# A graph layer's edge loop: TensorE's five steps in another order

## The chip, the cores and the metric

The kernel runs on one core of one Trainium2 chip. A core has five engines that run side by side, each through its own list of instructions in order: TensorE (PE; its weight loads are listed as PEld) multiplies matrices and writes to PSUM, VectorE (DVE) and ScalarE (ACT) do elementwise work, GpSimd (POOL) issues here the gathers by index, and SyncE (SP) issues the plain transfers. The metric is the time of one execution on the device in microseconds, as the median of several runs.

## The reference, cut to what matters

One layer of a graph transformer in float32: a message passing branch over 53,125 directed edges of 3,125 nodes with 256 features each, a linear attention branch, and a top-2 mixture of eight experts behind a second layer norm. The change touches the message passing branch alone. Cut to the terms that are not dropped, it computes:

```python
s0, s1 = _lin(x0[src], x1[src], ls0, ls1)          # gather of the source node
h0, h1 = _fctp(s0, s1, sh1, t1_00, t1_11, t1_01, t1_10)
h0, h1 = _lin(h0, h1, lh0, lh1)
sc = leaky_relu(h0) @ lsc * INV_MUL
act = softmax(concatenate([sc, zeros(E, 3 * 64)]))
o0, o1 = _fctp(h0, h1, sh1, t2_00, t2_11, t2_01, t2_10)
msgs = act * concatenate([o0, o1.reshape(E, 3 * 64)])
agg = segment_sum(msgs, dst)
```

The edges come sorted by destination. `sh1` is the unit vector of the edge, scaled.

## The kernel before, in words

Ahead of the loop the kernel normalises the nodes, folds the weight matrices into `wab` (first layer), `wo` (edge products) and `lsc` (second layer), and writes a table with one row of 448 numbers for each node. The edge loop (function `edges`) then works on 416 tiles of 128 edges, four tiles to a group, 104 groups. Behind it the expert blocks run, with TensorE as the busy engine.

For one group g the steps are:

- `gather` (L790, GpSimd): four indirect transfers fetch the rows of 4 x 128 source nodes into `xg`. There are seven `xg` buffers; one comes free when the group's sums are done.
- `features` (L813 to L815, VectorE): the dot product of the gathered vectors with the edge directions. Its last instruction is kept as `READY_[g]`.
- `places` (L798, L803, VectorE): 0/1 matrices `place` that say to which of 64 slots of a window of destinations each edge belongs; every third group also `move`, which carries a window into the next.
- `turn` (L820 TensorE, L822 ScalarE): four transposes into the PSUM tile `pz`, and a copy to `zT`.
- `products` (L830, L834, L838): the first layer `ph` on TensorE, from `zT` and `wab`, with 64 columns of the array for each half of the group; `little`, a scaled copy of it by ScalarE; and the edge products `eo`, four full multiplications of `zT` with `wo`. There are two `eo` buffers and one of `ph`.
- `second_layer` (L844, L850): VectorE takes the maximum `low` of `ph` and `little`, the leaky relu, and TensorE multiplies it with `lsc` to the scores `sc`, with 64 rows of the array for each half.
- `scores` (L858, L860): the minimum `nm` on VectorE, the exponentials `ex` and their sum on ScalarE.
- `messages` (L869 to L891): on VectorE the reciprocal `z` of the sum and the weight `zero` of the constant part; on ScalarE four scalings of `place` by `zero` into `zplace` (L876); on VectorE `oplace` (L878), and then the messages `msg` (L888 and L891), which read `eo`.
- `sums` (L914, L917, L921): TensorE adds `msg` and part of `xg` into the window's sum, with `oplace` and `zplace` as stationary matrices of 64 columns; in the last group of a window it also adds the part carried over from the window before (L921), ScalarE copies the first half of the sum out, and SyncE stores it to `agg` in memory.
- `second` (L937): in the last group of a window, TensorE carries from the first half to the second, which is copied out and stored in turn.

Pass s of the loop writes out, in this order: the gather of group s+3, the sums of s-3, one or two parts of side work (attention, and the routing of nodes to experts), the scores of s-2, features, places and transposes of s, the second layer of s-1, the messages of s-2, the products of s, and `second` of s-3. A planner turns this into one list for each engine: it takes the earliest written instruction that is ready by its own estimate of times, so that the lists can differ from the written order. `tc.issue_after(x)` pins the instructions of its block behind x in the list of their engine. The waits between engines follow from the data and the buffers.

Two such pins set TensorE's order before: the first layer of g comes behind the second layer of g-1 (`LSC[g - 1]`), and the second layer of g behind the transposes of g+1 (`TURN[g + 1]`). VectorE's pins put `low` of g behind the features of g+1 and the weight `z` of g behind `low` of g+1.

## Time and profile before

| what | value |
|---|---|
| median of 3 runs | 1110.63 us (1109.84 to 1115.06) |
| profiled execution | 1108.81 us |
| its span in the profile | 1106.9 us |
| edge loop in the span | from about 67 us (first gather) to 697 us |
| TensorE busy | 1018.8 us, 92% of the span |
| VectorE busy | 698.7 us, 63% |
| ScalarE busy | 500.6 us, 45% |
| GpSimd busy | 630.3 us, 57% |

A row of instructions in the profile gives the line of the kernel, the engine, the operation, the tile written and the tiles read, the shape and the number of instructions; behind the first bar the time they filled together and the mean of one in nanoseconds; behind the second the idle time of the engine just ahead of them and what ended it. On TensorE the shape begins with the part of the array in use: `128*64` is 128 rows by 64 columns. In the timelines the columns are start, length, engine, line, operation, tiles, shape and count, neighbouring instructions of one line being merged; the end of a matmul is modelled, so that it can lie behind the start of the next. In the table of stretches each engine has its busy time and its number of instructions, followed by the clock granted to TensorE, the busy share of the transfer engines, and GB/s.

### The profile page before, as it was taken

Reading aid. Unit: us, or ns where it says so; the run is one execution under the profiler, and the core shown is the slowest. Engines: PE = TensorE matmul, PEld = TensorE weight load, DVE = VectorE, ACT = ScalarE, POOL = GpSimd, SP = SyncE. Lnnn points to the kernel's source line nnn. Section 1 sums busy time; section 2 is a strip of 40 time slices with the busy share of each in tenths; the row PEclk is TensorE's granted clock in tenths of the full one; section 3 lists DMA queues with packets and bytes.
Section 4 is the critical chain, followed back from the end, with each engine's and each line's share of the span. In section 5 each row is a group of like instructions: output and inputs, shape, how many; then the busy total and the mean of one; then the engine's idle time right before and its main releaser. Section 6 shows DMA issues by size and latency. Waiting matters only on the chain.

```text
span 1106.9 us, 21729 instructions
## 1 busy us (share of the span) xinstructions
PE 1018.8 (92%) x7616; PEld 812.5 (73%) x7616; DVE 698.7 (63%) x2177; ACT 500.6 (45%) x1861; POOL 630.3 (57%) x623
## 2 busy tenths in 40 slices
PE   3848999999999999999999899899999999999996
PEld 3726776766667776776667676688888888888885
DVE  5987899988898989988888987322671111111110
ACT  3714556665576665765566545223211223222221
POOL 4447777777777776777766751432534434445322
PEclk9958999999999999999999899899999999999998
DMA  5945665667766686766766542765653667676651
GB/s 161 334 126 158 181 184 164 176 177 236 207 173 184 183 240 190 200 170 174 214 179 188 161 136 101 273 195 166 215 181 119 200 194 256 215 231 187 188 170 20
DMA packets 73882, 204.95 MB, mean 185 GB/s; under 512 B 13163, under 2 KB 48549, under 8 KB 70181
## 3 DMA queue, kind: packets, MB, share of 16 engines
q0 software_dynamic: 40736, 171.18, 52.9%
q1 hardware_dynamic: 31135, 30.40, 8.2%
q10 hardware_dynamic: 1894, 1.89, 0.5%
q8 instruction: 63, 1.03, 0.4%
q14 instruction: 54, 0.44, 0.1%
HBM read 176.00 MB, written 27.84 MB: 184 GB/s over the span
## 4 chain that ended last, share of the span: by engine, by line
PE 70%; DVE 12%; DMA 6%; issue 4%; POOL 3%; ACT 3%; SPq 0%; DVEq 0%; POOLq 0%; ACTq 0%
PE ps L1300 15%; PE ps L1318 15%; PE ps L917 8%; PE eo L838 7%; DMA xg<-table,srcT 4%; PE ph L830 4%; PE pz L820 3%; PE ps L914 3%; PE sc L850 3%; POOL xg L790 3%; PE gp L646 2%; PE gp L1095 2%; DVE tmp L813 2%; DVE msg L888 1%; PE ps L937 1%
## 5 line engine op out<-in xcount | busy, mean ns | idle before, releaser
L790 POOL DMA_INDIRECT xg<-table,srcT x416 | 441.1, 1060 | 163.5 <-issue 108.1
L876 ACT ACTIVATE zplace<-place,zero 128x64 f32<-128x64 f32 x416 | 115.3, 339 | 71.9 <-DVE zero L873 71.8
L838 PE MATMUL eo<-wo,zT 128*128 128x128 f32 x832 | 122.5, 292 | 25.3 <-DVE msg L891 24.9
L1305 ACT ACTIVATE hT<-ps,wt 128x256 f32<-128x256 f32 (+1 forms) x144 | 57.8, 453 | 194.3 <-issue 122.0
L838 PEld LDWEIGHTS eo<-wo,zT 128*128 128x128 f32 x832 | 105.4, 197 | 52.5 <-DVE msg L891 37.0
L860 ACT ACTIVATE ex<-sc,nm 128x65 f32<-128x65 f32 x416 | 125.5, 317 | 13.3 <-DVE nm L858 7.1
L1300 PE MATMUL ps<-xt,wt 128*128 128x256 f32 (+1 forms) x576 | 121.7, 368 | 4.4 <-DVE y L1321 4.4
L1318 PE MATMUL ps<-wt,hT 128*128 128x256 f32 x528 | 117.3, 379 | 0.0
L1300 PEld LDWEIGHTS ps<-xt,wt 128*128 128x128 f32 x576 | 103.4, 194 | 17.5 <-DVE y L1321 4.8
L813 DVE TENSOR_TENSOR tmp<-xg,r 128x768 f32<-128x768 f32 x104 | 98.7, 949 | 18.8 <-DMA xg<-table,srcT 15.4
L1318 PEld LDWEIGHTS ps<-wt,hT 128*128 128x128 f32 x528 | 98.8, 190 | 12.6
L917 PE MATMUL ps<-xg,zplace 128*64 128x192 f32 x832 | 107.5, 336 | 0.0
L1231 DVE COPY xt<-psx 128x512 f32<-128x512 f32 (+1 forms) x27 | 17.6, 651 | 140.1 <-PE psx L1230 133.2
L822 ACT COPY zT<-pz 128x512 f32<-128x512 f32 x104 | 60.7, 584 | 86.7 <-PE pz L820 85.1
L1323 POOL DMA_INDIRECT out_dram<-y,ridx_late x32 | 51.0, 1594 | 76.8 <-DVE y L1321 48.8
L917 PE MATMUL ps<-msg,zplace 128*64 128x192 f32 x692 | 91.4, 342 | 0.0
L860 ACT ACTIVATION_READ_ACCUMULATOR ex<-sc,nm 128x1 f32 x416 | 86.3, 208 | 0.0
L1323 POOL DMA_INDIRECT out_dram<-y,ridx_early x20 | 32.3, 1614 | 87.9 <-DVE y L1321 33.6
L820 PE MATMUL pz<-ident,xg 128*128 128x128 f32 x416 | 69.6, 288 | 10.4 <-DVE xg L815 8.1
L914 PE MATMUL ps<-msg,oplace 128*64 128x64 f32 (+1 forms) x832 | 78.4, 268 | 0.6 <-DVE msg L891 0.6
L820 PEld LDWEIGHTS pz<-ident,xg 128*128 128x128 f32 x416 | 45.3, 143 | 41.3 <-issue 32.9
L830 PE MATMUL ph<-zT,wab 128*64 128x256 f32 x416 | 69.0, 409 | 6.0 <-ACT zT L822 3.0
(383 smaller groups left out, 1898.3 us busy)
## 6 DMA issues: line engine op xcount, KB each, us to landing
xg<-table,srcT POOLq DMA_INDIRECT x416, 3.7
table<-xt SPq DMA_DIRECT2D x4, 1120.0 KB
agg<-win SPq DMA_DIRECT2D x70, 64.0 KB
agg<-zero SPq DMA_DIRECT2D x1, 3200.0 KB
x<-in_x_dram SPq DMA_DIRECT2D x2, 768.0 KB
at<-agg SPq DMA_DIRECT2D x2, 768.0 KB
out_dram<-x SPq DMA_DIRECT2D x2, 768.0 KB
rows<-at SPq DMA_DIRECT2D x2, 768.0 KB
```

The lines of the kernel that those rows point to most:

```text
L790: nc.gpsimd.indirect_dma_start(out=XG[g][:, i, :], out_offset=None, in_=table[:, :], in_offset=bass.IndirectOffsetOnAxis(ap=srcT[:, j:j + ...
L813: nc.vector.tensor_mul(tmp, xg[:, :, U:D].rearrange("p g (m u) -> p g m u", m=3), rbc(g))
L820: TURN[g] = nc.tensor.transpose(pz[:, i, :], XG[g][:, i, 0:P], ident)
L830: nc.tensor.matmul(ph[h * U:(h + 1) * U, :], lhsT=wab, rhs=zT[:, 2 * h:2 * h + 2, :].rearrange("p t e -> p (t e)"), start=True, stop=True)
L838: nc.tensor.matmul(eo[:, t, :], lhsT=zT[:, t, :], rhs=wo, start=True, stop=True)
L860: nc.scalar.activation(ex[:, i, :], sc[:, i, 0:U + 1], AF.Exp, scale=-1.0, bias=nm[:, i:i + 1], accum_out=z[:, i:i + 1])
L876: nc.scalar.activation(zero_place[:, i, :], place[:, i, :], AF.Copy, scale=zero[:, i:i + 1])
L914: nc.tensor.matmul(ps[hs, 0:c1], lhsT=one_place[:, i, :], rhs=msg[:, i, 0:c1], start=whole, stop=False)
L917: nc.tensor.matmul(ps[hs, U:D], lhsT=zero_place[:, i, :], rhs=msg[:, i, U:D] if what == 1 else xg[:, i, D:TW], start=False, stop=False)
L1300: nc.tensor.matmul(ps[:, h, 0:W_], lhsT=w[:, k * HID + cc * P:k * HID + (cc + 1) * P], rhs=xT[:, k, 0:W_], start=(k == 0), stop=(k == 1))
L1318: nc.tensor.matmul(ps, lhsT=hT[:, cc, s * P:(s + 1) * P], rhs=w[:, o:o + D], start=(cc == 0), stop=(cc == NC - 1))
L1323: nc.gpsimd.indirect_dma_start(out=out[:, :], out_offset=bass.IndirectOffsetOnAxis(ap=ridx[q][:, at_], axis=0), in_=y[:, s, :], in_offset= ...
```

## The change

TensorE's cycle becomes: sums of s-3, first layer and edge products of s-1, transposes of s, second layer of s-1, `second`. For that `products` moves from group s to group s-1 and ahead of `turn`; the first layer of g is pinned behind the last sum of g-2 (`SUMS`), the edge products behind the first layer, the transposes of g behind the edge products of g-1 (`WO`), and `second` of g behind the second layer of g+2. `messages` is split: the weights with `oplace` and `zplace` are now a function `weights`, written ahead of `products`; the messages proper stay behind the second layer. On VectorE `z` of g is pinned behind the features of g+2, `low` of g behind `oplace` of g-1 (`PLACED`), and the messages of g behind `low` of g+1 as before. `places` moves to the end of the pass. The diff, shortened:

```diff
             def turn(g):
                 pz = zps.tile([P, G, P], F32, name="pz")
-                for i in range(G):
-                    TURN[g] = nc.tensor.transpose(pz[:, i, :], XG[g][:, i, 0:P], ident)
+                with tc.issue_after(WO[g - 1].ins) if g else nullcontext():
+                    for i in range(G):
+                        TURN[g] = nc.tensor.transpose(pz[:, i, :], XG[g][:, i, 0:P], ident)
...
                 for h in range(2):
-                    with tc.issue_after(LSC[g - 1].ins) if g and not h else nullcontext():
-                        nc.tensor.matmul(ph[h * U:(h + 1) * U, :], lhsT=wab,
+                    with tc.issue_after(SUMS[g - 2].ins) if g >= 2 and not h else nullcontext():
+                        first = nc.tensor.matmul(ph[h * U:(h + 1) * U, :], lhsT=wab,
...
                 for t in range(G):
-                    nc.tensor.matmul(eo[:, t, :], lhsT=zT[:, t, :], rhs=wo, start=True, stop=True)
+                    with tc.issue_after(first.ins) if not t else nullcontext():
+                        WO[g] = nc.tensor.matmul(eo[:, t, :], lhsT=zT[:, t, :], rhs=wo, start=True, stop=True)
...
-                with tc.issue_after(READY_[g + 1].ins) if g + 1 < NG else nullcontext():
+                with tc.issue_after(PLACED[g - 1].ins) if g else nullcontext():
                     LOW[g] = nc.vector.tensor_tensor(low, ph, little, OP.max)
...
-            def messages(g):
-                eo, place = EO.pop(g), S.pop(g)
-                ex, z = HEAD.pop(g)
-                order = LOW[g + 1] if g + 1 < NG else None
-                with tc.issue_after(order.ins) if order else nullcontext():
+            def weights(g):
+                place = S.pop(g)
+                ex, z = HEAD[g]
+                with tc.issue_after(READY_[g + 2].ins) if g + 2 < NG else nullcontext():
                     nc.vector.scalar_tensor_tensor(z, ex[:, :, U], float(3 * U - 1), z, op0=OP.mult, op1=OP.add)
...
-                order = nc.vector.tensor_mul(one_place, place, z.unsqueeze(2).to_broadcast([P, G, W]))
+                PLACED[g] = nc.vector.tensor_mul(one_place, place, z.unsqueeze(2).to_broadcast([P, G, W]))
+                MSG[g] = one_place, zero_place
+
+            def messages(g):
+                eo = EO.pop(g)
+                ex, z = HEAD.pop(g)
+                one_place, zero_place = MSG.pop(g)
+                order = LOW[g + 1] if g + 1 < NG else PLACED[g]
...
-                    ENDS[v] = nc.tensor.matmul(SUM[v][W:P, :], lhsT=MOVE.pop(v)[0:W, 1, :], rhs=WIN[v][0:W, :],
-                                               start=False, stop=True)
+                    with tc.issue_after(LSC[g + 2].ins) if g + 2 < NG else nullcontext():
+                        ENDS[v] = nc.tensor.matmul(SUM[v][W:P, :], lhsT=MOVE.pop(v)[0:W, 1, :],
+                                                   rhs=WIN[v][0:W, :], start=False, stop=True)
...
                 if s < NG:
                     features(s)
-                    places(s)
+                if 2 <= s < NG + 2:
+                    weights(s - 2)
+                if 1 <= s < NG + 1:
+                    products(s - 1)
+                if s < NG:
                     turn(s)
                 if 1 <= s < NG + 1:
                     second_layer(s - 1)
                 if 2 <= s < NG + 2:
                     messages(s - 2)
                 if s < NG:
-                    products(s)
+                    places(s)
```

More of the change, by code (lines that the diff above doesn't have):

```diff
@@ L771, in edges @@
             XG, S, ZT, EO, MSG, WIN, SUM, MOVE = {}, {}, {}, {}, {}, {}, {}, {}
-            READY_, HEAD, LOW, LSC, TURN, SC, M1 = {}, {}, {}, {}, {}, {}, {}
+            READY_, HEAD, LOW, LSC, TURN, SC, WO, PLACED, SUMS = {}, {}, {}, {}, {}, {}, {}, {}, {}
             ENDS = {}
@@ L828, in products @@
                 for h in range(2):
-                    with tc.issue_after(LSC[g - 1].ins) if g and not h else nullcontext():
-                        nc.tensor.matmul(ph[h * U:(h + 1) * U, :], lhsT=wab,
-                                         rhs=zT[:, 2 * h:2 * h + 2, :].rearrange("p t e -> p (t e)"),
-                                         start=True, stop=True)
+                    with tc.issue_after(SUMS[g - 2].ins) if g >= 2 and not h else nullcontext():
+                        first = nc.tensor.matmul(ph[h * U:(h + 1) * U, :], lhsT=wab,
+                                                 rhs=zT[:, 2 * h:2 * h + 2, :].rearrange("p t e -> p (t e)"),
+                                                 start=True, stop=True)
                 little = ew.tile([P, 2 * P], F32, name="little")
@@ L916, in sums @@
                                 else:
-                                    nc.tensor.matmul(ps[hs, U:D], lhsT=zero_place[:, i, :],
+                                    SUMS[g] = nc.tensor.matmul(ps[hs, U:D], lhsT=zero_place[:, i, :],
                                                      rhs=msg[:, i, U:D] if what == 1 else xg[:, i, D:TW],
@@ L920, in sums @@
                 if q == n - 1:
-                    nc.tensor.matmul(ps[0:W, :], lhsT=MOVE[v][:, 0, :], rhs=WIN.pop(v - 1),
-                                     start=False, stop=True)
+                    SUMS[g] = nc.tensor.matmul(ps[0:W, :], lhsT=MOVE[v][:, 0, :], rhs=WIN.pop(v - 1),
+                                               start=False, stop=True)
                     WIN[v] = spool.tile([P, D], F32, name="win", bufs=3)
@@ L936, in second @@
                 if q == n - 1:
-                    ENDS[v] = nc.tensor.matmul(SUM[v][W:P, :], lhsT=MOVE.pop(v)[0:W, 1, :], rhs=WIN[v][0:W, :],
-                                               start=False, stop=True)
+                    with tc.issue_after(LSC[g + 2].ins) if g + 2 < NG else nullcontext():
+                        ENDS[v] = nc.tensor.matmul(SUM[v][W:P, :], lhsT=MOVE.pop(v)[0:W, 1, :],
+                                                   rhs=WIN[v][0:W, :], start=False, stop=True)
                     close(v, 1)
```

## The prediction

> **What bounds the kernel now.** I read the page first, then the busy time by stretches, then the timelines of a clean stretch, then GpSimd's waits.
>
> ```profile
> span 1106.9 us, 21729 instructions
> PE 1018.8 (92%) x7616; PEld 812.5 (73%) x7616; DVE 698.7 (63%) x2177; ACT 500.6 (45%) x1861; POOL 630.3 (57%) x623
> ...
> L790 POOL DMA_INDIRECT xg<-table,srcT x416 | 441.1, 1060 | 163.5 <-issue 108.1
> ...
> L838 PE MATMUL eo<-wo,zT 128*128 128x128 f32 x832 | 122.5, 292 | 25.3 <-DVE msg L891 24.9
> ```
>
> The whole-span shares mislead: the edge loop fills only 78 to 697 us; after it TensorE runs the expert blocks, which the change doesn't touch and which only shift. 104 groups of four edge tiles pass through the loop, 5.9 us each. Within it three engines are nearly full:
>
> ```profile
> core 0: us, PE busy (x) PEld busy (x) DVE busy (x) ACT busy (x) POOL busy (x), PEclk, DMA share, GB/s
> ...
> 200.00:260.00 60.00, 58.84 (x578) 41.92 (x577) 54.32 (x157) 39.70 (x168) 45.41 (x44) 1.00 0.64 174
> ...
> 545.00:660.00 115.00, 106.54 (x970) 79.07 (x972) 103.27 (x355) 67.24 (x286) 76.46 (x75) 0.95 0.61 169
> ```
>
> In the clean stretch (200 to 260 us, no side work) TensorE is at 98% and VectorE at 91%; where the gate is mixed in (545 to 660) VectorE is at 90%. GpSimd looks idle for a quarter, but isn't: every gather is followed by 0.30 us in which it waits for nothing shown. 441.1 us of gathers plus 415 such pauses (127 us) are 568 us out of the 591 between the first gather and the last. So the gather stream has a pace of its own, 4 x (1.06 + 0.30) = 5.45 us a group, and TensorE, at 5.03 in the clean stretch (twelve groups from 200.1 to 260.4), is faster there than its supply.
>
> **What the order costs.** One group on TensorE, with the tile shape in each row (columns: start, length, line):
>
> ```profile
> 234.93 0.34 PE L914 MATMUL ps<-msg,oplace 128*64 128x64 f32 x4
> ...
> 236.61 0.66 PE L820 MATMUL pz<-ident,xg 128*128 128x128 f32 x4
> 237.20 0.66 PE L850 MATMUL sc<-lsc,low 64*128 64x65 f32 x8
> 237.94 0.65 PE L830 MATMUL ph<-zT,wab 128*64 128x256 f32 x4
> 238.53 1.16 PE L838 MATMUL eo<-wo,zT 128*128 128x128 f32 x8
> 239.62 0.34 PE L914 MATMUL ps<-msg,oplace 128*64 128x64 f32 x4
> ```
>
> From start to start: sums 1.68, transposes 0.59, second layer 0.74, first layer 0.59, edge products 1.09; together 4.69. The shape changes at all five borders. A stretch in which the transposes stand directly ahead of the edge products, both 128*128, shows the price of one border:
>
> ```profile
> 374.01 0.66 PE L820 MATMUL pz<-ident,xg 128*128 128x128 f32 x4
> 374.50 1.06 PE L838 MATMUL eo<-wo,zT 128*128 128x128 f32 x8
> 375.49 0.34 PE L914 MATMUL ps<-msg,oplace 128*64 128x64 f32 x4
> ```
>
> Transposes here take 0.49 instead of 0.59. Single starts agree: from one edge product to the next 0.112 us, from the last one to the sums 0.205; from sum to sum 0.156, from the last sum to the transposes 0.256. A change of shape costs 0.093 to 0.100.
>
> **The change, part by part.** The new cycle is sums (128*64), first layer (128*64), edge products (128*128), next transposes (128*128), second layer (64*128). Two borders go: sums to first layer, 0.10, and edge products to transposes, 0.09; 0.19 a group. The border from second layer to sums takes the place of that from second layer to first layer, both 64*128 to 128*64 (0.202 at its shortest). But today that border takes 0.354 in most clean groups, since the first layer waits for the copy of zT, with only the second layer between; after the change the sums lie between too, so 0.15 more goes in a plain group. In every third group the carry matmul (L937) stands there and already covers the copy. So: plain group 4.69 - 0.34 = 4.35; third group 5.70 (239.62 to 245.32, start of the sums to the next) - 0.19 = 5.51; mean 4.74 instead of 5.03. Saved 0.29 a group, 30 us over 104 groups, if TensorE were alone.
>
> [...]
>
> Nothing is added: no instruction, buffer or transfer; the split of the messages step (weights, then products) issues the same small VectorE operations and four ScalarE scalings (L876). Moving the slot compare (place) last on VectorE costs nothing, 0.34 us that fits anywhere in a group of 4.9. The carry, pinned behind the second layer, already ran there. Its store and the others on SP's queue stay in order and nothing reads them until a gate batch. GpSimd's queue keeps its gathers; it is moved past nothing, and xg is freed 1.7 us earlier in the cycle, since the sums come ahead of the first layer and the edge products.
>
> **Where a gain can land.** Features of a group can't start before its gather has landed. In this trace that distance (start of L813 less landing) falls to 0 at groups 47 to 52 and 70 to 76; there a faster TensorE only waits. It can gain before them only what GpSimd itself lost by waiting for buffers. GpSimd's waits from 100 to 472 us:
>
> ```profile
> POOL xg L790 <- issue: 60.3, 198, 0.3
> POOL xg L790 <- PE pz L820: 11.8, 17, 3.1
> ...
> POOL xg L790 <- PE ps L917: 2.5, 4, 0.9
> ```
>
> Less the regular 0.30 of each, all waits sum to 8.1 us. So up to group 76 at most 8 us come in; I take 7, since 76 x 0.29 = 22 is on offer. After it the gathers run 7 to 18 us ahead at the last nine groups and GpSimd's own lost waits are 15.9 us, so supply no longer limits; 28 groups x 0.29 = 8.1. But VectorE is at 90% there with its gate work, and some of TensorE's 8 us of idle time are its waits for messages. I count half: 4. The ceiling is 8 + 8 = 16 us, plus about 1 us of the drained pipeline at the end, from the earlier sums.
>
> [...]
>
> Sum: 1108.81 us (profiled execution, 1106.9 span and 1.9 around it) - 11 = 1097.8. The median of the runs shown is 1.8 above the profiled one: **1099.6 us**.
>
> **A wait that could appear.** In the new VectorE order the maximum of the first layer (low) is pinned behind the placement weights, and it needs the ScalarE copy little, which shares ScalarE's in-order queue with the four scalings. The present rows (233 to 240 us):
>
> ```profile
> 236.38 0.15 DVE L873 TENSOR_TENSOR zero<-z,ex 128x4 f32<-128x4 f32 x1
> ...
> 236.56 0.59 ACT L876 ACTIVATE zplace<-place,zero 128x64 f32<-128x64 f32 x2 [1.06 <-DVE zero L873]
> 237.30 0.59 ACT L822 COPY zT<-pz 128x512 f32<-128x512 f32 x1 [0.15 <-PE pz L820]
> 237.79 0.58 ACT L876 ACTIVATE zplace<-place,zero 128x64 f32<-128x64 f32 x2
> 238.70 0.39 ACT L834 ACTIVATE little<-ph 128x256 f32<-128x256 f32 x1 [0.33 <-PE ph L830]
> ```
>
> With little first: sums 1.58, first layer 0.65, hand-over 0.11, little 0.41, low 0.34, messages 0.87 + 0.41, hand-over 0.05: 4.42 us, about TensorE's own 4.35, and harmless. With the scalings first the ring is nm 0.41 + 0.10, exp 1.30 + 0.06, weights 0.31 + 0.03, scalings 1.06, little 0.41, low 0.34, messages 1.28: 5.30 us. Which comes first is fixed when the program is built, by which is ready earlier in the planner's view. Counted from the start of the sums, the first layer ends at 2.23; the zero weight is ready at 0.36 + 0.10 + 1.30 + 0.06 + 0.31 = 2.13, or 2.2 behind the features, later still behind side work. The trace can't settle it.
>
> **The rivals.** (A) Borders saved, supply limits the first three quarters: 1099.6, own range 1092 to 1105; 55%. For it: borders measured at single starts, 98% busy TensorE. Against: VectorE's 90%. (B) The order is as announced but VectorE and the gathers swallow it, gain 0 to 4: 1109; 13%. For it: the zero distance at two places. Also here: the planner already puts transposes ahead of the edge products in some 25 groups, where only one border is left to save. (C) Slower: the scalings stand ahead of little in most groups, a ring of 5.30 us. It decides when the zero weight is ready over 0.1 us before the first layer ends. The 45 or so groups that now run near 5.03 lose 0.27, 12 us; and then the other groups, with side work in the gaps, gain next to nothing: 1110.6 + 12 = 1123, and 1114 where it strikes half of them; 28%. [...]
>
> **Chances.** Half a per cent, 5.6 us, is about what a measurement can tell. Faster: nearly all of A and D, 0.56. Within: B and a quarter of C, 0.18. Slower: 0.26. The range has to reach into C's middle: 1091 to 1123, leaving out half of D and about half of C.
>
> **What would show it.** Right: eo directly followed by pz 0.11 us later, sums by ph 0.16 later, clean groups of 4.35 until features wait for DMA (L813's wait for xg grows from 15 us to over 25), GpSimd's waits for pz and ps nearly gone up to 470 us. Wrong: a long wait of low for little, and of the scores matmul (L850) for low; clean groups at 5.3; GpSimd waiting for ps more than now.

## The result, and the profile after

| | before | after |
|---|---|---|
| median | 1112.0 us (1109.84 to 1115.06, 4 runs) | 1223.7 us (1219.14 to 1226.23, 4 runs) |
| ratio to before | | 1.0998, interval 1.0952 to 1.1044 |
| span of the profiled execution | 1106.9 us | 1217.0 us |
| last scores matmul of the loop starts at | 688.3 us | 797.6 us |

The change makes the kernel 10% slower. All of it lies in the edge loop: its end moves by 109.3 us and the span by 110.1; from there to the end of the span it is 419 us in both. The page of after, in the lines that answer those shown of before, with the features added:

```profile
span 1217.0 us, 21711 instructions
PE 1032.5 (85%) x7616; PEld 841.7 (69%) x7616; DVE 705.6 (58%) x2177; ACT 506.8 (42%) x1861; POOL 623.7 (51%) x623
...
L790 POOL DMA_INDIRECT xg<-table,srcT x416 | 433.8, 1043 | 281.7 <-PE ps L925 107.1
...
L840 PE MATMUL eo<-wo,zT 128*128 128x128 f32 x832 | 122.9, 291 | 0.0
...
L813 DVE TENSOR_TENSOR tmp<-xg,r 128x768 f32<-128x768 f32 x104 | 99.5, 956 | 131.0 <-DMA xg<-table,srcT 130.3
```

None of these operations became dearer: the features take 956 ns each (949 before), an edge product 291 (292), a gather 1043 (1060). What grew is idle time, on three engines at once. One line of the waits of before (engine, tile, line, what it waited for: us in total, times, longest us), and then the chain of waits of after:

```profile
DVE tmp L813 <- DMA xg<-table,srcT: 15.4, 12, 2.2
```

```profile
DVE tmp L813 <- DMA xg<-table,srcT: 130.3, 56, 6.1
POOL xg L790 <- PE ps L925: 107.1, 38, 7.5
PE sc L852 <- DVE low L846: 99.2, 45, 6.2
PEld ps L922 <- ACT win L937: 24.0, 29, 1.3
DVE low L846 <- ACT little L835: 21.0, 24, 2.1
```

Read from top to bottom, the first three close a circle. VectorE's features wait for the gathers. The gathers wait for TensorE's sums, which free the `xg` buffers. TensorE waits for `low`, which is VectorE's. Each engine is idle because the next one is, and none of the three is full. The stretches of after say the same; of before, TensorE was at 98% in the first of them and at 93% in the second:

```profile
core 0: us, PE busy (x) PEld busy (x) DVE busy (x) ACT busy (x) POOL busy (x), PEclk, DMA share, GB/s
200.00:260.00 60.00, 45.53 (x425) 34.02 (x424) 41.99 (x117) 29.50 (x127) 39.43 (x39) 0.91 0.57 153
...
545.00:660.00 115.00, 91.65 (x846) 70.01 (x842) 83.33 (x277) 58.85 (x251) 68.27 (x67) 0.93 0.56 158
```

**Where the circle sits.** The next three views are timelines of the same 18 us: VectorE, GpSimd, TensorE (start, length, engine, line, operation, tiles, shape, count, idle time before it):

```profile
279.84 0.96 DVE L813 TENSOR_TENSOR tmp<-xg,r 128x768 f32<-128x768 f32 x1 [0.99 <-DMA xg<-table,srcT]
...
283.05 0.95 DVE L896 TENSOR_TENSOR msg<-eo,r 128x768 f32<-128x768 f32 x1
...
289.56 0.97 DVE L813 TENSOR_TENSOR tmp<-xg,r 128x768 f32<-128x768 f32 x1 [4.45 <-DMA xg<-table,srcT]
...
291.94 0.41 DVE L846 TENSOR_TENSOR low<-ph,little 128x256 f32<-128x256 f32 x1
292.27 0.94 DVE L896 TENSOR_TENSOR msg<-eo,r 128x768 f32<-128x768 f32 x1
```

```profile
282.03 0.94 POOL L790 DMA_INDIRECT xg<-table,srcT  x1 [4.76 <-DVE zero L874]
...
285.79 0.94 POOL L790 DMA_INDIRECT xg<-table,srcT  x1 [0.31 <-issue]
...
297.13 2.08 POOL L790 DMA_INDIRECT xg<-table,srcT  x1 [5.11 <-PE ps L925]
```

```profile
292.40 1.12 PE L852 MATMUL sc<-lsc,low 64*128 64x65 f32 x8 [4.31 <-DVE low L846]
293.59 0.48 PE L922 MATMUL ps<-msg,oplace 128*64 128x64 f32 x4
...
295.99 0.85 PE L925 MATMUL ps<-xg,zplace 128*64 128x192 f32 x4
```

Counted from the start of the loop, the features at 289.56 are those of group 36, `low` at 291.94 is group 32's, and the messages at 292.27 are group 31's. So in VectorE's list the features of a group stand ahead of the messages of the group **five** before it; call this distance the lead. The list runs in order, so the messages of 31, whose inputs were there by 286.2 us, stood still until the rows of group 36 had landed. `low` of 32, whose `little` was ready at 287.05, stood behind the same features, and TensorE waited for it. The rows of 36 were fetched late for want of a buffer: gather 36 (282.03) needs the buffer of group 29, whose last sum ends at 281.75 (the view names `zero`), and gather 38 (297.13) that of 31. Follow it once around. First to last gather of group 36: 3.76 us. Last gather to features: 3.77. Features, weights, `low` and the two message products of 31, to 293.53: 3.97. Sums of 31, to 296.84: 3.31. Hand-over: 0.29. Together 15.10 us, at the end of which the gathers are **two** groups further: 7.55 us a group, against 5.9 before.

That gives a rule for this loop. With n buffers and a lead of d, one turn of the circle brings n - d groups. As estimates from this one turn of 15.1 us: a lead of 3 with seven buffers gives 3.8 us a group, less than the gather stream's own pace of 5.45, and the circle isn't felt; a lead of 4 gives 5.0, about at that pace; a lead of 5 gives 7.55 and sets the pace of everything. The trace of after bears this out inside one run: from the first gather of a group to that of the next it takes 5.63 us in the mean where the lead is 3, 5.81 where it is 4, and 7.63 where it is 5. Counted in the traces, the features of before had a lead of 2 in 23 groups, 3 in 60 and 4 in 19; those of after 3 in 24, 4 in 19 and 5 in 58. The time from the features of a group to its first sum went from 23.7 us (median of groups 25 to 99) to 40.1.

Neither kernel has a pin that keeps features behind messages. Where they stand is the planner's choice when it builds the lists, and with the new pins it chose earlier places, up to two short of the seven buffers. Why the planner chose them is not on record.

### The profile page after: what moved, and what is told of

Same layout as the page of the kernel before. It is cut to its first block, busy times and chain, and to the rows that moved or that the text cites. A ratio compares the mean times of both kernels' runs of the same rounds, so it can differ in the third digit from the quotient of the medians.

```text
span 1217.0 us, 21711 instructions
## 1 busy us (share of the span) xinstructions
PE 1032.5 (85%) x7616; PEld 841.7 (69%) x7616; DVE 705.6 (58%) x2177; ACT 506.8 (42%) x1861; POOL 623.7 (51%) x623
## 5 line engine op out<-in xcount | busy, mean ns | idle before, releaser
L790 POOL DMA_INDIRECT xg<-table,srcT x416 | 433.8, 1043 | 281.7 <-PE ps L925 107.1
L813 DVE TENSOR_TENSOR tmp<-xg,r 128x768 f32<-128x768 f32 x104 | 99.5, 956 | 131.0 <-DMA xg<-table,srcT 130.3
L852 PE MATMUL sc<-lsc,low 64*128 64x65 f32 x832 | 75.6, 305 | 99.2 <-DVE low L846 99.2
L877 ACT ACTIVATE zplace<-place,zero 128x64 f32<-128x64 f32 x416 | 110.4, 337 | 114.2 <-DVE zero L874 113.7
L852 PEld LDWEIGHTS sc<-lsc,low 64*128 64x128 f32 x832 | 60.4, 205 | 120.2 <-DVE low L846 111.2
L925 PE MATMUL ps<-xg,zplace 128*64 128x192 f32 x832 | 117.8, 366 | 0.0
L922 PE MATMUL ps<-msg,oplace 128*64 128x64 f32 (+1 forms) x832 | 84.5, 286 | 25.6 <-DVE msg L899 13.6
L925 PE MATMUL ps<-msg,zplace 128*64 128x192 f32 x692 | 99.1, 369 | 0.0
L922 PEld LDWEIGHTS ps<-msg,oplace 128*64 128x64 f32 x832 | 56.6, 153 | 57.6 <-ACT win L937 24.0
L831 PE MATMUL ph<-zT,wab 128*64 128x256 f32 x416 | 83.8, 413 | 0.8 <-issue 0.8
L925 PEld LDWEIGHTS ps<-xg,zplace 128*64 128x64 f32 x832 | 67.9, 156 | 18.3 <-issue 3.0
```

Source lines behind the costliest of these rows:

```text
L790: nc.gpsimd.indirect_dma_start(out=XG[g][:, i, :], out_offset=None, in_=table[:, :], in_offset=bass.IndirectOffsetOnAxis(ap=srcT[:, j:j + ...
L813: nc.vector.tensor_mul(tmp, xg[:, :, U:D].rearrange("p g (m u) -> p g m u", m=3), rbc(g))
L831: first = nc.tensor.matmul(ph[h * U:(h + 1) * U, :], lhsT=wab, rhs=zT[:, 2 * h:2 * h + 2, :].rearrange("p t e -> p (t e)"), start=True, st ...
L852: LSC[g] = nc.tensor.matmul(sc[:, 2 * h + b, 0:U + 1], lhsT=low[hs, b * P:(b + 1) * P], rhs=lsc[hs, :], start=True, stop=True)
L877: nc.scalar.activation(zero_place[:, i, :], place[:, i, :], AF.Copy, scale=zero[:, i:i + 1])
L922: nc.tensor.matmul(ps[hs, 0:c1], lhsT=one_place[:, i, :], rhs=msg[:, i, 0:c1], start=whole, stop=False)
```

## The experiments

Two theories came out of the trace. **Theory 1**: the lead. The features were hoisted in VectorE's list, and the loss is the circle above. **Theory 2**: the carry. `second` (L946) now directly precedes the next sums in TensorE's list; they write the same PSUM tile and wait for ScalarE's copy of the window, a start to start of 0.83 us where 0.31 follows when nothing is to be waited for. In after the sums follow it directly 23 times of 35; 35 times 0.52 would be 18 us. The rivals are those of the prediction: VectorE's new order as such, the gathers' supply, TensorE's order.

The kernels ran on different chips, each beside the kernel before. On two of them the kernel before, too, took 6 to 7% longer (1190.74 and 1176.97 us, where it took 1110.98 to 1113.2 on the others). Ratios are therefore taken to the kernel before on the same chip, and what ran on those two is marked **(slow chip)**. The changed kernel itself ran on neither of the two, so that sizes there can't be set against its 1.10; what their traces show comes at the end.

| kernel | lead of the features: groups | time, us | ratio to before |
|---|---|---|---|
| before | 2: 23, 3: 60, 4: 19 | 1112.0 | |
| pin4_c, features held | 2: 4, 3: 98 | 1103.22 | 0.9904 (0.9875 to 0.9933) |
| before_pin, features held | 2: 24, 3: 78 | 1106.99 | 0.9941 (0.9920 to 0.9962) |
| vehalf | 3: 38, 4: 53, 5: 9 | 1139.96 | 1.0256 (1.0186 to 1.0326) |
| xg8, eight buffers | 4: 19, 5: 26, 6: 40 | 1206.28 | 1.0832 (1.0748 to 1.0917) |
| after_b | 3: 24, 4: 19, 5: 58 | 1221.45 | 1.1011 (1.0936 to 1.1087) |
| pehalf (slow chip) | 4: 5, 5: 93 | 1331.29 | 1.1195 (1.1115 to 1.1274) |
| hoist (slow chip) | 5: 98 | 1408.84 | 1.1854 (1.1764 to 1.1945) |

The pace by lead is the same in the other traces. On the usual chips the groups with a lead of 5 take 7.64 us in `after_b`, 7.46 in `sec_b` and 7.69 in `vehalf`, where they are only 9 of the 104; those with a lead of 3 take 5.64 to 5.75. The runs follow in turn.

### The lead alone, taken away: pin4

One pin holds the features of g behind the last message product of g-4. Nothing else of the source is touched. The planner builds all lists anew, though, and with the pin VectorE's and ScalarE's lists differ from those of the changed kernel in more than the place of the features:

```diff
-                nc.vector.tensor_mul(tmp, xg[:, :, U:D].rearrange("p g (m u) -> p g m u", m=3), rbc(g))
+                with tc.issue_after(DONE[g - 4].ins) if g >= 4 else nullcontext():
+                    nc.vector.tensor_mul(tmp, xg[:, :, U:D].rearrange("p g (m u) -> p g m u", m=3), rbc(g))
...
-                nc.vector.tensor_mul(msg[:, :, 0:U], eo[:, :, 0:U], ex[:, :, 0:U])
+                DONE[g] = nc.vector.tensor_mul(msg[:, :, 0:U], eo[:, :, 0:U], ex[:, :, 0:U])
```

It ran first on a slow chip:

> The changed kernel with one pin more: the features of group g (L813) come behind the last message instruction of group g-4 in VectorE's list, as in most groups of the kernel before, where 3 groups of messages were outstanding; the planner left to itself put them ahead of the messages of g-5. Theory 1 (features too early in VectorE's list, so that messages and sums, which free the gather buffers, stand behind a wait for a gather): the loop comes back to about the pace of the kernel before, 1095 to 1120 us, waits of L813 for gathers fall from 130 to under 40 us, waits of the scores matmul for low from 99 to under 20. Theory 2 (TensorE's new order or the pin of low behind the placement weights is itself the loss): stays over 1180 us.

1217.46 us, ratio 1.0209 (1.0124 to 1.0294). The time lies in the range named for theory 2, but the ranges were set for a kernel before of 1112 us; beside one of 1190.74 it is 2% above, not 10%. L813's waits fell to 5.1 us, as theory 1 had it, those of the scores for `low` to 30.0, not under 20. And again on another slow chip:

> The changed kernel with the features of g held behind the messages of g-4, and the carry left where the change put it. Theory 1 as the main cause and theory 2 as the rest: between the kernel before and the changed one and near the former, ratio 1.01 to 1.03; less pin4sec's 0.999 this is the carry's price, 12 to 30 us. L813 waits for xg under 20 us; the sums wait for win about 20 us. If the carry costs nothing, the ratio is 0.995 to 1.003.

1205.27 us, ratio 1.0225 (1.0157 to 1.0294). On a usual chip, in the square of four described below:

> Features held, carry last. Theory 1 as the main cause: ratio 1.01 to 1.03. If the carry is the main cause: 1.06 or more.

1103.75 us, ratio 0.9934 (0.9907 to 0.9961): lower than either expectation, and below the kernel before. The hold takes back the whole loss and more.

### The carry, and both together: the square of four

`sec` moves the carry from the end of the pass to behind the edge products; `pin4sec` has both edits.

```diff
-                    with tc.issue_after(LSC[g + 2].ins) if g + 2 < NG else nullcontext():
+                    with tc.issue_after(WO[g + 2].ins) if g + 2 < NG else nullcontext():
                         ENDS[v] = nc.tensor.matmul(SUM[v][W:P, :], lhsT=MOVE.pop(v)[0:W, 1, :],
...
                     products(s - 1)
+                if 3 <= s:
+                    second(s - 3)
...
-                    second(s - 3)
```

On a slow chip, the carry alone:

> The changed kernel with the carry matmul (L946, second) behind the edge products instead of behind the second layer, so that the ScalarE copy of its result has the transposes and the second layer as cover before the next sums, which now wait 0.53 us for it in 35 groups. VectorE's list is unchanged. Theory 1 (features): the ring stays, and at most 35 x 0.53 = 18 us come off: 1200 to 1224. Theory 3 (the carry's copy is the main loss): under 1180.

1252.23 us, ratio 1.0504 (1.0430 to 1.0578), above both ranges in time; by its ratio it would lie in the range of theory 3 (1180 of 1112 us is 1.06). The same edit on a usual chip, `sec_b` below, has 1.0957, so this chip doesn't decide it. On a usual chip, both edits, with the changed kernel beside them:

> The changed kernel with both suspected costs undone: the features of g held behind the messages of g-4, and the carry issued behind the edge products. If theory 1 and theory 2 together are the whole loss, the ratio to before falls to 0.98 to 1.00, L813's waits for xg to under 20 us and the waits of the sums for win to under 5 us. If VectorE's new order itself (low behind the next group's weights) costs as the rival of the prediction had it, the ratio stays at 1.02 or above and sc waits for low over 60 us.

1110.09 us, ratio 0.9989 (0.9955 to 1.0024).

> The changed kernel as it stands, beside the other kernels of this call. Ratio to before 1.08 to 1.12 by both theories. Theory 1 (the features of a group stand in VectorE's list ahead of the messages of five groups earlier, so that only two groups are in flight through the seven xg buffers): L813 waits for xg about 130 us. Theory 2 (the carry at the end of TensorE's list makes the next sums wait for the window's copy): the sums that follow a carry wait about 0.5 us each, 35 times.

1222.18 us, ratio 1.1001 (1.0896 to 1.1107); L813 waited for `xg` 132.2 us. With both undone together the loss is gone, but that doesn't say which of the two did it. So all four corners ran side by side on one chip:

> The changed kernel, as the first corner of a square of four on one chip: features free or held, carry last or behind the edge products. Ratio to before 1.08 to 1.11 by every theory.

> Features free, carry behind the edge products. Theory 1 as the main cause: the ratio stays at 1.05 to 1.10, and L813 waits for xg over 90 us. If the carry is the main cause: 1.03 or less.

> Features held and carry behind the edge products. If both costs are real and add up: lowest of the four, 0.99 to 1.01. If one of them is none: no lower than the better of the two that undo one.

| | carry last | carry behind the edge products |
|---|---|---|
| features free | 1221.45 us, 1.1011 (1.0936 to 1.1087) | 1217.17 us, 1.0957 (1.0894 to 1.1019) |
| features held | 1103.75 us, 0.9934 (0.9907 to 0.9961) | 1108.04 us, 0.9982 (0.9947 to 1.0016) |

The rows differ by 118 and 109 us, the columns by 4.3 us in opposite directions. Theory 1 stands and theory 2 falls: moving the carry alone leaves the loss. The waits of the corner with the carry moved and the features free show why it doesn't help:

```profile
DVE tmp L813 <- DMA xg<-table,srcT: 125.6, 51, 5.5
...
POOL xg L790 <- PE ps L925: 103.3, 40, 6.9
...
PE sc L852 <- DVE low L846: 87.7, 40, 6.1
...
PEld ps L922 <- ACT win L937: 5.4, 8, 0.7
```

The waits for `win` did go, from 24.6 us to 5.4, while the circle is as it was. With the features held, the same waits (20.0 us of weight loads) cost nothing that their removal gives back: moved, the carry leaves sums that wait for messages instead (21.0 us on TensorE, 14.9 without the move).

### The lead alone, put into the kernel before: hoist

TensorE's order, and VectorE's otherwise, stay as before. Features are written three passes earlier, and one more pin makes the weight z of g wait for the features of g+5:

```diff
+                if s == 0:
+                    for g in range(3):
+                        features(g)
+                if s + 3 < NG:
+                    features(s + 3)
                 if s < NG:
-                    features(s)
...
-                with tc.issue_after(order.ins) if order else nullcontext():
+                with tc.issue_after(order.ins) if order else nullcontext(), \
+                        tc.issue_after(READY_[g + 5].ins) if g + 5 < NG else nullcontext():
```

> The kernel before, TensorE's pins and VectorE's other pins untouched, with the features of group g written three passes earlier and the weight z of g-5 pinned behind them, so that VectorE's list has the features of g ahead of the messages of g-5 throughout. Theory 1: a ring over two groups, gathers (5.0) + landing (2.5) + features, weights, low, messages, sums (about 7) in two groups, 7 to 7.5 us a group instead of 5.9: 1200 to 1260 us, with long waits of GpSimd for the sums. Theory 2: 1105 to 1120, since TensorE's order is the old one.

1408.84 us, ratio 1.1854 (1.1764 to 1.1945), with a lead of 5 in 98 groups (slow chip): in the direction of theory 1, and beyond its range. The circle's two waits, in the order before:

```profile
DVE tmp L813 <- DMA xg<-table,srcT: 226.9, 97, 5.2
POOL xg L790 <- PE ps L918: 219.0, 42, 11.7
```

So the kernel before gets the same two waits with none of the change's pins on TensorE, from an edit that only moves features ahead of messages. `pin4` takes the loss away by an edit that only moves them back. That is shown by the pins; the lists of the other engines, which the planner built along with them, were not held fixed.

### Either half of the change alone: pehalf and vehalf

`pehalf` has TensorE's new order with VectorE's pins as before. `vehalf` has VectorE's new pins and the split of the messages, with TensorE's order as before.

```diff
# pehalf
-                with tc.issue_after(PLACED[g - 1].ins) if g else nullcontext():
+                with tc.issue_after(READY_[g + 1].ins) if g + 1 < NG else nullcontext():
                     LOW[g] = nc.vector.tensor_tensor(low, ph, little, OP.max)
...
-                with tc.issue_after(READY_[g + 2].ins) if g + 2 < NG else nullcontext():
+                with tc.issue_after(LOW[g + 1].ins) if g + 1 < NG else nullcontext():
                     nc.vector.scalar_tensor_tensor(z, ex[:, :, U], float(3 * U - 1), z, op0=OP.mult, op1=OP.add)
...
```

```diff
# vehalf
-                    with tc.issue_after(SUMS[g - 2].ins) if g >= 2 and not h else nullcontext():
+                    with tc.issue_after(LSC[g - 1].ins) if g and not h else nullcontext():
...
-                if 1 <= s < NG + 1:
-                    products(s - 1)
...
+                    products(s)
                     places(s)
...
```

> TensorE's half of the change alone: sums, first layer, edge products, transposes, second layer, with VectorE's pins as before (low behind the features of the next group, z behind low). In the built lists the features stand ahead of the messages of g-5 in nearly all groups. Theory 1: as slow as the whole change or slower, 1210 to 1260 us. Theory 2b (the new pins of VectorE cause the loss): under 1130 us.

1331.29 us, ratio 1.1195 (1.1115 to 1.1274), lead 5 in 93 groups; L813 waited for `xg` 171.2 us (slow chip). As slow as the whole change or slower, as theory 1 had it, though above its range in time.

> VectorE's half of the change alone, with TensorE's order as before. The features stand four groups ahead of the messages in half of the groups and three in most others, so the ring through the xg buffers covers three groups or more. Theory 1: the ratio lies between before and the changed kernel, 1.02 to 1.07, with L813 waiting for xg 40 to 90 us. If the place of features doesn't matter and VectorE's order is what costs, the ratio is that of the changed kernel, 1.08 or more, with under 30 us of waits of L813; if TensorE's order is what costs, 0.99 to 1.01.

1139.96 us, ratio 1.0256 (1.0186 to 1.0326), lead 4 in 53 groups and 5 in 9. Its waits lie between those of before and after, as theory 1 has it:

```profile
DVE tmp L813 <- DMA xg<-table,srcT: 47.7, 33, 3.9
...
POOL xg L790 <- PE ps L923: 36.4, 11, 8.6
```

So either half alone makes the planner hoist the features, TensorE's half the more. With `pin4` beside it, the new order on TensorE isn't what is slow; what is slow is VectorE's list as the planner builds it beside that order.

### One buffer more: xg8

```diff
-        with tc.tile_pool(name="xgp", bufs=7) as xgp, tc.tile_pool(name="sp", bufs=5) as spool, \
+        with tc.tile_pool(name="xgp", bufs=8) as xgp, tc.tile_pool(name="sp", bufs=5) as spool, \
...
-                tmp = ew.tile([P, G, 3, U], F32, name="tmp")
+                tmp = ew.tile([P, G, 3, U], F32, name="tmp", bufs=1)
```

> The changed kernel with eight xg buffers in place of seven (one buffer of tmp in place of two pays for the space). Theory 1: the features move one place further ahead with the buffer (six groups ahead of the messages in a third of the groups, five in a fifth), so two groups stay in flight and the ratio stays within 0.03 of that of the changed kernel, with L813 waiting for xg over 80 us. Rival (the gathers just lack a buffer): the ratio falls to 1.03 or below and the waits for xg to under 40 us.

1206.28 us, ratio 1.0832 (1.0748 to 1.0917), 16 us less than the changed kernel beside it. L813 still waited for `xg` 108.2 us. The edit also takes one of the two `tmp` buffers, to pay for the space. With the eighth `xg` buffer the lead is 6 in 40 groups, and 8 - 6 is again two groups a turn; in the other groups three or more are left, and the time is lower. One buffer more gives back 16 us of 109.

### The supply of gathers, and a shorter lead

These ran on a slow chip, beside `pin4_again`. `before_sp` and `pin4sec_sp` fill the fourth tile of each group by a plain transfer, and so leave out the lookup of a quarter of the edges:

```diff
+                    if i == G - 1:
+                        row = j * P % (N - P)
+                        nc.sync.dma_start(XG[g][:, i, :], table[row:row + P, :])
+                        continue
                     nc.gpsimd.indirect_dma_start(
```

> The kernel before with the fourth gather of each group left out: its tile is filled from 128 consecutive rows of the table by a plain transfer that SyncE issues, so GpSimd has three gathers of 1.06 us a group in place of four. It leaves out the lookup of a quarter of the edges. If GpSimd's supply bounds the loop (the prediction's rival A), the loop gains until TensorE bounds it: ratio 0.97 to 0.99. If VectorE or TensorE bounds it already, 0.99 to 1.01.

1166.62 us, ratio 0.9896 (0.9859 to 0.9933).

> The changed kernel with both costs undone, and the same fourth gather of each group replaced by a plain transfer (it too leaves out the lookup of a quarter of the edges). If GpSimd's supply is what ate TensorE's saving of 19 us, this kernel is 10 to 25 us faster than the same edit of the kernel before (ratio of the two 0.978 to 0.99). If VectorE's list is what eats it, the two are within 5 us of each other.

1181.84 us, ratio 1.0035 (1.0009 to 1.0060): 15 us slower than `before_sp`, where it was to be faster or equal. With other rows the nodes are routed otherwise and the expert blocks grow (640 matmuls at their first line instead of 576; some 470 us between the loop and the end instead of 419), so the whole times don't compare with kernels that have all their gathers. The ends of the loops do: 697.8 us in `before_sp` and 716.3 in `pin4sec_sp`, where `pin4_again`, with all gathers, has 784.0 on the same chip. For the kernel before there is no trace of that chip; from its 1176.97 us, less the 419 behind the loop and 2 around the span, I estimate 756. So the loop of the kernel before loses some 58 us when a quarter of the gathers leaves GpSimd's queue, which speaks for the supply as its bound on this chip. It isn't what puts the changed order behind there: that stays 18.5 us later with the supply loosened. The next run loses on this chip too:

> As the kernel with both costs undone, but the features of g held behind the messages of g-3, a group further back. Theory 1: a shorter list ahead of the messages leaves the gathers a group more of room, L813 no longer waits for xg at all; VectorE then has the features late for the transposes instead, and TensorE waits for them: ratio 0.99 to 1.01. If distance from the gathers were all that counts, 0.985 or below.

1209.17 us, ratio 1.0276 (1.0213 to 1.0340), above the range expected. The hold here is behind the messages of g-3, a lead of 2 throughout. L813's waits fell to 3.4 us, but the run is confounded by the chip: `pin4_again` beside it had 1.0225. Whether a lead of 2 costs anything on a usual chip was not tried.

### What the order is worth once the lead is held: before_pin

`pin4` was faster than the kernel before, which itself has a lead of 4 in 19 groups. Is the gain the new order's, or only the hold's? The kernel before got the same pin as `pin4`:

> The kernel before with the same hold on the features (behind the messages of g-4). In its list only 19 groups of 104 stood four ahead of the messages. If the hold merely takes back what the change's list lost, this kernel is the kernel before, ratio 0.997 to 1.003, and what the held version of the changed kernel gains is TensorE's order and VectorE's. If the hold itself is the gain, the ratio is 0.993 or less, like that kernel's.

> The changed kernel with the features held, beside the kernel before with the same hold. Ratio to before 0.990 to 0.997; its lead over the held kernel before is the worth of the change without the hoist, 4 to 11 us.

| | time, us | ratio to before |
|---|---|---|
| before_pin | 1106.99 (1105.29 to 1108.72, 9 runs) | 0.9941 (0.9920 to 0.9962) |
| pin4_c | 1103.22 (1100.81 to 1103.85, 6 runs) | 0.9904 (0.9875 to 0.9933) |

Both: the hold by itself gives the kernel before 6.2 us (1113.2 less 1106.99), between the two ranges expected, and the order with the hold 3.8 us on top, just short of the 4 to 11. The two sets of runs don't overlap, though the intervals of their ratios do. Held, the changed kernel is the fastest of all that ran.

The page of `pin4_c` and its waits, and then one plain group of its TensorE, from the sums of one group to those of the next:

```profile
span 1101.3 us, 21704 instructions
...
L790 POOL DMA_INDIRECT xg<-table,srcT x416 | 441.9, 1062 | 153.4 <-issue 108.9
```

```profile
PE sc L853 <- DVE low L847: 18.4, 20, 7.0
PE ps L923 <- DVE msg L900: 14.6, 25, 2.2
...
DVE tmp L814 <- DMA xg<-table,srcT: 13.2, 9, 2.6
...
PE ps L923 <- ACT win L938: 9.1, 20, 0.5
...
POOL xg L790 <- PE ps L926: 6.4, 9, 3.4
```

```profile
228.78 0.34 PE L923 MATMUL ps<-msg,oplace 128*64 128x64 f32 x4
...
230.36 0.60 PE L832 MATMUL ph<-zT,wab 128*64 128x256 f32 x4
230.89 1.16 PE L841 MATMUL eo<-wo,zT 128*128 128x128 f32 x8
231.89 0.60 PE L822 MATMUL pz<-ident,xg 128*128 128x128 f32 x4
232.42 0.66 PE L853 MATMUL sc<-lsc,low 64*128 64x65 f32 x8
233.55 0.34 PE L923 MATMUL ps<-msg,oplace 128*64 128x64 f32 x4 [0.47 <-DVE msg L900]
```

This is the order of the change as the prediction had it: 4.77 us from sums to sums, 0.47 of them waiting for the messages, 4.30 without. The next group, which has the carry, takes 6.20 (233.55 to 239.75), with 0.36 of waiting for `low` and 0.46 for `win`: 5.38 without. Predicted were 4.35 and 5.51.

But the groups don't keep that pace. Where the prediction counted 5.03 us a group for the kernel before and forecast 4.74, between 200 and 260 us, the held kernel's take 5.26 in the mean, and its TensorE is at 91% there. The two stretches of before and of the held kernel that follow tell how much arrives over the loop; the first row is that clean stretch of the held kernel, the second the loop of before, the third the loop of the held kernel:

```profile
200.00:260.00 60.00, 54.45 (x563) 41.98 (x559) 53.34 (x155) 39.65 (x170) 46.89 (x44) 1.00 0.64 175
```

```profile
80.00:690.00 610.00, 575.37 (x5318) 422.02 (x5320) 532.21 (x1685) 365.31 (x1546) 433.70 (x410) 0.97 0.64 181
```

```profile
80.00:690.00 610.00, 555.12 (x5360) 430.43 (x5359) 538.55 (x1691) 373.55 (x1555) 435.10 (x410) 0.97 0.64 181
```

In this stretch TensorE is busy 20.3 us less, but it ends at a fixed time, when the held kernel is further on. Over the same work, from the first transposes to the last sum of the loop, it is busy 557.7 us instead of 580.9, 23.2 less, and idle 55.6 instead of 35.8, 19.8 more. The idle time has new places: gone are the waits of the edge products for messages (24.9 us before) and of the first layer for zT (3.0); come are those of the scores for `low` (18.4), of the sums for messages (14.6) and for `win` (9.1). The last scores move from 688.3 to 682.9, by 5.4 us.

By GpSimd's rows, what holds the rest back is the supply that the prediction named. Beyond its work and its regular 0.30 us pauses GpSimd lost 26.2 us in before and 16.1 in the held kernel; the last gather starts 8.9 us earlier (648.7 instead of 657.7). From group 24 to group 84 the gathers run at one pace in both, 5.59 and 5.60 us a group, with less than 10 us lost in 336. How far the held kernel's messages run ahead of those of before agrees: 5.1 us at group 24, not at all at group 66, 6.8 at group 96. That doesn't grow by 0.29 a group. A run with a faster supply on a usual chip, which would settle it, was not made.

## Why the prediction was wrong, point by point

The forecast was 1099.6 us and faster; the time was 1223.7, outside the range and on the other side.

**The step that failed** is the sentence that begins "Nothing is added: no instruction, buffer or transfer", with the end of its paragraph, that `xg` is freed 1.7 us earlier in the cycle. As a list of operations it is right, and so is "GpSimd's queue keeps its gathers; it is moved past nothing". But it priced VectorE's new list by its operations and left the place of the features where it was. The features did move, by one to two groups ahead of the messages, and this changed how far GpSimd can run: from four groups a turn to two. `xg` was freed later, not earlier: from the features of a group to its first sum went 40.1 us instead of 23.7. The cost is seen on the queue that was "moved past nothing": between its first and last gather, the time beyond its work and its regular 0.30 us pauses went from 26.2 to 146.3 us. The prediction had the warning in hand: for ScalarE it said that which instruction comes first "is fixed when the program is built, by which is ready earlier in the planner's view", and asked it only of the scalings and `little`. None of the rivals had this mechanism.

**"Features of a group can't start before its gather has landed. In this trace that distance falls to 0 at groups 47 to 52 and 70 to 76; there a faster TensorE only waits."** This was right as far as the supply goes, and left out the lead. Groups 45 to 52 and 69 to 76 are two of the three places where the kernel before has a lead of 4 (the third is groups 89, 91 and 92). Ahead of groups 45 to 60 GpSimd lost less than 1 us beyond its work and its pauses, and less than 2 ahead of 69 to 80: the circle wasn't closed there, the gathers ran at their own pace. In `before_pin`, where the lead is 3, they come no earlier (the first gather of group 76 starts at 492.4 us, in before at 492.2). What the lead changed is who stood still: with a lead of 4 the features of these groups start 3.4 to 5.4 us behind the start of their last gather and the messages wait behind them, in `before_pin` 5.5 to 9.1 us behind it. So these two places show the first leg of the circle, messages held up by a wait for a gather, without the second, gathers held up by sums. The prediction took the wait for TensorE's alone and didn't ask what a lead of 5 would do, though the buffers (7) and each leg of the circle stood in the rows.

**"The change of shape costs 0.093 to 0.100" and "0.19 a group".** Right. In after, an edge product is followed by the transposes 0.112 us later and the last sum by the first layer 0.156 later, where a border costs 0.20 to 0.26; 104 x 0.19 = 20 us, and TensorE's busy time over the loop of the held kernel fell by 23.2, of which the last 3 are not explained. The 0.15 of the zT wait went from its place, but the border took other waits: from the last scores to the sums it is 0.202 at its shortest and 0.57 in the median of the held kernel's 43 that follow each other directly.

**"At most 8 us come in" up to group 76, 11 in all.** In the changed kernel nothing came in. With the lead held, 5.4 us at the loop's end and 3.8 us against the held kernel before. There the messages of group 76 start 3.0 us earlier than before, where 7 were predicted, and those of group 100 6.5 earlier, where 11 were: the sign was right for that kernel, the size about twice too large, and the limit by supply, at most 8 us up to group 76, held. That the held kernel's 0.9904 matches the forecast's 0.990 is luck: 6.2 us of it are the hold's, which the change doesn't have. D is counted in the chances with a gain of over 18 us; no run shows it. The largest gain of a kernel with the new order is 10.0 us (1113.2 less the 1103.22 of `pin4_c`), and its gathers keep the pace of before from group 24 to group 84, 5.60 us a group and 5.59.

**"The carry, pinned behind the second layer, already ran there."** It did, but what followed changed: the first layer before, sums into the same PSUM tile now. The wait that this brings is real (24.0 us of weight loads in after), and the square shows that moving the carry away from it gains nothing that counts: 4.3 us in one row, and 4.3 lost in the other.

**Rival C**, the slower one, asked for the scalings ahead of `little` and a long wait of `low` for it. In after that order came in 11 of 103 groups; in the others ScalarE ran `little` first. `low` waited for `little` 21.0 us in all (10.9 before), 2.1 at most. Its end, slower, was right by luck: the mechanism was another. Two signs named against the forecast did come, the long wait of the scores for `low` (99.2 us) and GpSimd's longer waits for the sums (107.1 us); the cause of the first was that `low` stood behind features. And "L813's wait for xg grows from 15 us to over 25" was named as a sign that the forecast is right; it grew to 130.3. A sign that both a success and a failure produce is a poor one.

## What to carry to other kernels

Where a planner builds the lists, a change of order on one engine can move instructions of another that the edit doesn't name. Before pricing such a change, list for every engine whose instructions consume a buffered supply how far they stand ahead of those that free the buffers: one turn of the circle divided by the buffers less that lead is the time a group can't beat (here 15.1 us by 2, 7.55, where 7.63 were measured), and a lead without a pin above it isn't a constant. When it grows, hold it with a pin; here another buffer let it grow by one more in 40 groups.

## What was not expected of the hardware

**Behind a wait of 4.31 us TensorE ran at half clock, and the circle pays for it.** In after TensorE is idle for 4.31 us up to 292.40. The stretches of one microsecond, with the granted clock as the third number from the end:

```profile
291.00:292.00 1.00, 0.00 (x0) 0.00 (x0) 1.00 (x6) 0.29 (x2) 1.00 (x1) 0.91 0.73 168
292.00:293.00 1.00, 0.60 (x6) 0.60 (x8) 1.00 (x3) 1.00 (x5) 0.02 (x1) 0.50 0.71 174
...
298.00:299.00 1.00, 1.00 (x6) 0.53 (x5) 0.39 (x1) 1.00 (x6) 1.00 (x1) 0.68 0.00 0
```

The clock is at 0.50 from about 291.8 to 298.6, and the sums of that group take 3.25 us from the first start to the last end, where those of the group ahead of it take 1.75 at full clock (284.38 to 286.13): 1.5 of the circle's 15.1 us. TensorE stopped at 288.1; the clock fell 3.7 us later and came back after 6.2 us of work. From 90 us to the end of the loop the clock of after stands at half for 123 us in 24 stretches of 3.4 or 6.8 us, that of before for 31 us in 8. The matmuls with `xg` and `zplace` take 366 ns in the mean in after (L925) and 336 in before (L917). In after they take 525 ns inside these stretches and 326 between them, so the row's growth comes from the half clock.

**Chips differ.** On the two slow chips the tail behind the loop takes what it takes elsewhere (419 us for `pin4_again`, 418 for `pin4_c`), and rows such as the edge product (298 ns against 290) and the gather (1031 against 1062) are nearly the same; yet the loop of the held kernel ends at 784 instead of 683. The traces there show engines that start late where the profile shows no wait: pauses of over 0.6 us inside the loop that it puts down to "issue" sum to 30.0 us on TensorE and 26.1 on VectorE in `pin4_again`, none and 11.6 in `pin4_c`; after a carry the sums start 1.48 us later in the median, instead of 0.83. What delays them is open, and so is why the held kernel loses to the kernel before there (1.0225) and gains on it elsewhere (0.9904): of the kernel before there is no trace on those chips.
